# Loads of delta * u regrouped by partition quarters, and B multiplied half a unit ahead

## The chip, the cores and the metric

The kernel runs on one core of a Trainium2 chip. The metric is the device time of one execution in microseconds, as the median of several runs. The engines are TensorE (PE, with its weight loads as PEld), VectorE (DVE), ScalarE (ACT), GpSimd (POOL) and SyncE (SP). SyncE issues most of the transfers here, which sixteen DMA engines carry out.

## The reference, cut to what matters

A model of four layers. Layers 0 and 1 are selective scans over images of 64 x 64 positions with 96 channels, widened to 192 channels (E), 16 states (NS) and 4 scan directions (K), for 4 images. Layers 2 and 3 are attention and feed-forward layers on tokens, which the change doesn't touch. The core of layers 0 and 1 is, for each image, direction k and channel e:

```python
delta = softplus(einsum('bkrl,kdr->bkdl', dts, dt_w) + bias)
def step(h, inp):                       # over the L = 4096 positions
    u, d, b, c = inp
    dA = exp(d[..., None] * A)
    h = dA * h + d[..., None] * b[:, :, None, :] * u[..., None]
    y = einsum('bken,bkn->bke', h, c)
    return (h, y)
```

So for each channel and state: a decay exp(delta * A), a drive delta * u * B, a first-order recurrence along the positions, and a sum over the states with C.

## The kernel before, in words

Two images are worked on at a time (a pair), so there are four phases: two layers times two pairs. A phase consists of `prepare` (normalisation, convolution, the projections; it writes delta, delta * u, B and C to DRAM), of `scan_phase`, and of `finish` (which overlaps the next `prepare`). After the four phases, `token_layers` computes layers 2 and 3.

In `scan_phase` a partition stands for one state of one of G = 8 groups (4 directions of 2 images): 16 x 8 = 128 partitions. Partition 32a + 4g + s holds group g and state 4a + s. The free axis holds time in chunks of TC = 512 positions. The work is cut into units: one chunk and EB = 12 channels. There are 8 chunks of 16 units, 128 units in a phase, 512 in all. For each unit:

- `load` fetches delta * u from DRAM to the tile `h`, 128 x 12 x 512 in float32, each row of a group copied to all of its 16 states' partitions: 3 MB. Before, it does that in six transfers of 512 KB: three sets of four channels, each for partitions 0 to 63 and for 64 to 127 (line 390). The DRAM tensor `du` holds every row twice (its first dimension of 2), so that the source of one half has 16 different rows, each of which is read four times. `load` first calls `load_delta`, which fetches delta as three bfloat16 parts for 8 groups, 24 rows, to the tile `dlt` (line 375).
- `times_b` multiplies h by B on GpSimd, three channels at a time, four times in a unit (line 401).
- `replicate` spreads delta over the 128 partitions by a matmul to PSUM (line 407), and `decay` turns it into exp(delta * A) on ScalarE (line 411).
- `scan` runs the recurrence on VectorE for one channel, in place in h (line 418).
- `contract` sums over the states with C on TensorE (line 436), `evict` copies the sums out on ScalarE (line 448), and `store` sends them to DRAM in four transfers of 48 KB (line 456).

The order is written out by hand, and every engine executes its instructions in the order of the text. The loop goes over units and within them over the 12 channels. At channel n of unit `at` it replicates four channels ahead (LEAD), decays three ahead, scans channel n, and contracts a part of the unit before. `b_at` placed the B products of unit `at` + 1 there, one whole unit ahead. After the last channel it stores the unit before and loads unit `at` + 3; the h tiles have four buffers, so this load goes to the buffer that the unit before has just left. `weights` (line 359, ScalarE) prepares the matmul weights of the next chunk from C; `load_b` and `load_c` fetch B and C of a chunk, 16 partitions times 8 groups in four transfers of 32 partitions (line 343).

All of these transfers are issued by SyncE. At most eight are under way: each waits for the one eight issues earlier (eight completion semaphores in turn).

Of the kernel before, what the change touches and what calls it, by code (L numbers as in the profile page):

```python
# [11 lines left out]
BF16 = mybir.dt.bfloat16  # L12
# [12 lines left out]
NS = 16  # L25
R = 6
K = 4
G = 2 * K
PAD = HW + 2
TC = 512  # L30
NC = L // TC
ROWS = TC // HW
EB = 12
NEB = E // EB
ER = EB // 4
PITCH = 2
NP16 = 3
# [3 lines left out]
NF = HID // 128  # L41
EPS = 1e-5
LEAD = 4
LN_EXP = "natural_log_exp_and_others"
SQRT_HALF = 0.7071067811865476

# [33 lines left out]
class Consts:  # L80
# [3 lines left out]
    def load(self, pool, name, shape):  # L84
        t = pool.tile(shape, F32, name=name)
        self.nc.sync.dma_start(t, self.a[name])
        return t
# [39 lines left out]
class Scans:  # L127
# [19 lines left out]
    def prepare(self, ph):  # L147
# [16 lines left out]
        with self.tc.tile_pool(name="prep", bufs=1) as wp, self.tc.tile_pool(  # L164
# [3 lines left out]
            def load(name, shape, at=0):  # L168
                t = wp.tile([at + shape[0]] + shape[1:], F32, name=name)
                nc.sync.dma_start(t[at:], a[pre + name])  # L170
                return t

            xp = load("x_proj", [C, 2, 2, XD2])
            dt_w = load("dt_w", [XD2 - 2 * NS, 2, E], at=2 * NS)
            conv_b = load("conv_b", [C, 2])
            ds = load("Ds", [C, 2, K])
            dsum = wp.tile([C, 2], F32, name="dsum")
# [192 lines left out]
    def load_delta(self, u):  # L370

        nc, ph = self.nc, u.ph
        u.dl = self.units.tile([64 + NP16 * G, EB, TC], BF16, name="dlt", bufs=3)
        at = u.eb * EB
        nc.sync.dma_start(
            u.dl[64:].rearrange("p e t -> p (e t)"),
            ph.delta[u.c][:, :, at : at + EB].rearrange("n g e t -> g n (e t)"),
        )

    def load(self, u):  # L380

        nc, ph = self.nc, u.ph
        u.h = self.units.tile([128, EB, TC], F32, name="h", bufs=4)
        self.load_delta(u)
        n = 4
        for e in range(0, EB, n):
            for half in range(2):
                at = u.eb * EB + e
                part = slice(64 * half, 64 * half + 64)
                nc.sync.dma_start(  # L390
                    u.h[part, e : e + n].rearrange("p e t -> p (e t)"),
                    ph.du[u.c][:, :, at : at + n]
                    .rearrange("a g e t -> (a g) (e t)")
                    .unsqueeze(1)
                    .broadcast_to([2 * G, NS // 4, n * TC]),
                )

    def times_b(self, u, r):
        h = u.h[:, ER * r : ER * r + ER]
# [3 lines left out]
    def replicate(self, u, n):  # L403

        u.a[n] = self.p_a.tile([128, TC], F32, name="a")
        rep = self.cst.rep[64 : 64 + NP16 * G]
        self.nc.tensor.matmul(u.a[n], rep, u.dl[64:, n], start=True, stop=True)  # L407

    def decay(self, u, n):
        at = u.eb * EB + n  # L410
# [50 lines left out]
    def scan_phase(self, ph):  # L461

        nc = self.nc
        units = [self.Unit(ph, c, eb) for c in range(NC) for eb in range(NEB)]
        last = len(units)

        def ahead(t, do):
            at, n = divmod(t, EB)  # L470
            if at < last:
                do(units[at], n)

        def b_at(t):
            at, n = divmod(t, EB)
            if n % ER == 0 and 0 <= at + 1 < last:
                self.times_b(units[at + 1], n // ER)

        with self.tc.tile_pool(name="units", bufs=2) as self.units, self.tc.tile_pool(
            name="p_a", bufs=6, space=PSUM  # L480
        ) as self.p_a, self.tc.tile_pool(name="p_y", bufs=2, space=PSUM) as self.p_y:
            with self.tc.manual_schedule():
                self.start_phase(ph)
                self.load_b(ph, 0)
                self.load(units[0])
                self.load_c(ph, 0)
                self.load(units[1])
                self.load(units[2])
                self.load_c(ph, 1)
                for t in range(-EB, 0, ER):  # L490
                    b_at(t)
                for op in range(16):
                    self.weights(ph, 0, op)
                for t in range(LEAD):
                    ahead(t, self.replicate)
                for t in range(LEAD - 1):
                    ahead(t, self.decay)
                for at, u in enumerate(units):
                    before = units[at - 1] if at else None
                    for n in range(EB):  # L500
                        t = at * EB + n
                        ahead(t + LEAD, self.replicate)
                        ahead(t + LEAD - 1, self.decay)
                        self.scan(u, n)
                        q, part = divmod(n, 3)
                        if before:
                            if part < 2:
                                self.contract(before, q, part)
                            else:
                                self.evict(before, q)  # L510
                            if n == 4 and before.c < NC - 1:
                                e = before.eb * EB
                                nc.scalar.copy(
                                    ph.carry[:, e : e + EB], before.h[:, :, TC - 1]
                                )
                        b_at(t)
                        if n == 1 and u.eb >= 2 and u.c + 1 < NC:
                            self.weights(ph, u.c + 1, u.eb - 2)
                        if n == 7 and u.eb >= NEB - 2 and u.c + 1 < NC:
                            self.weights(ph, u.c + 1, u.eb)  # L520
                        if n == EB - 1:
                            if before:
                                self.store(before)
                            if u.eb == 8 and u.c + 1 < NC:
                                self.load_b(ph, u.c + 1)
                            if u.eb == NEB - 1 and u.c + 2 < NC:
                                self.load_c(ph, u.c + 2)
                            if at + 3 < last:
                                self.load(units[at + 3])
                for q in range(4):  # L530
                    self.contract(units[-1], q, 0)
                    self.contract(units[-1], q, 1)
                    self.evict(units[-1], q)
                self.store(units[-1])
# [178 lines left out]
def token_layers(ctx: ExitStack, tc, cst, a, layers, x_in, x_out):  # L713
# [51 lines left out]
    def layernorm(t, cut, out, first, **quant):  # L765
# [6 lines left out]
        with ExitStack() as order:  # L772
# [4 lines left out]
            if first:  # L777
                nc.scalar.preload_act_table_set(LN_EXP)
        var = p_a.tile([128, TC], F32, name="pa")
# [199 lines left out]
```

## Time and profile before

| | |
|---|---|
| median of 3 runs | 12560.81 us (12543.26 to 12572.67) |
| the profiled execution: time, span | 12532.27 us, 12530.5 us |
| mean granted TensorE clock | 0.736 |
| busy share of the span: PE, DVE, ACT, POOL | 78%, 75%, 56%, 59% |
| the four scan phases, first to last scan | 772 to 2728, 3655 to 5582, 6517 to 8460, 9394 to 11333 us |
| bytes moved | 2491.55 MB, of them 2163.45 on SyncE's queue |

The page's second section cuts the span into 40 slices with the busy share of each engine in tenths. Its fifth section lists groups of instructions: busy time in us and mean ns of one, then the idle time of the engine just before them and what ended most of it. In a table by stage each engine has its busy us and, in brackets, its instructions; the last three columns are the granted clock, the mean busy share of the sixteen DMA engines, and GB/s. In a list of waits, "A <- B: t, n, m" says that A stood t us in total, n times and m us at most, until B was done.

### The profile page before, as it was taken

To read this page: it belongs to the slowest core of one execution; us is meant where nothing else is said; L and a number is where in the kernel's file an instruction comes from. 1 tells how busy PE (TensorE), PEld (TensorE's weight loads), DVE (VectorE), ACT (ScalarE), POOL (GpSimd) and SP (SyncE) were. 2 spreads that over 40 slices of the span, in tenths; PEclk is the share of its full clock that TensorE was granted. 3 is DMA by queue.
4 is the path that set the end of the run, shared out by engine and by line. 5 is a ranking of instruction groups with operands and counts; after the bars stand their busy time and mean duration, and the time that the engine had idled before them with its cause. 6 is when DMAs were issued, how large, how long until landed. Compare 5 with 4: busy or idle time off the path is not lost.

```text
span 12530.5 us, 341384 instructions
## 1 busy us (share of the span) xinstructions
PE 9786.3 (78%) x147008; PEld 4985.2 (40%) x147008; DVE 9408.2 (75%) x9235; ACT 7029.5 (56%) x11815; POOL 7413.5 (59%) x2316
## 2 busy tenths in 40 slices
PE   7757788769878878869877788877877878777777
PEld 2224444433334444433334444443334444444333
DVE  2479999972569999982569999992459999994567
ACT  2356666643456666653456666662446666663456
POOL 0159888860149999870139989880118999991000
PEclk8667766679777776769777776768776676778887
DMA  3689999974679999984579999994569999994100
GB/s 93 174 223 246 239 240 242 241 183 130 201 210 248 246 248 242 243 204 125 179 206 246 244 244 245 241 227 126 159 203 236 246 245 245 246 241 134 32 21 10
DMA packets 964628, 2491.55 MB, mean 199 GB/s; under 512 B 295442, under 2 KB 578224, under 8 KB 753840
## 3 DMA queue, kind: packets, MB, share of 16 engines
q1 hardware_dynamic: 634416, 2163.45, 66.2%
q10 hardware_dynamic: 328704, 306.26, 8.4%
q8 instruction: 1158, 18.97, 0.7%
q14 instruction: 350, 2.87, 0.1%
HBM read 1955.42 MB, written 513.80 MB: 197 GB/s over the span
## 4 chain that ended last, share of the span: by engine, by line
PE 31%; DMA 28%; issue 6%; DVE 5%; SPq 4%; ACT 4%; POOL 1%; ACTq 0%; DVEq 0%; POOLq 0%
DMA h<-du 24%; PE y L436 8%; PE c L259 6%; PE a L407 5%; SPq L390 3%; PE f L586 3%; PE d L305 2%; DMA yk<-y 1%; DVE h L418 1%; PE c L288 1%; PE f L595 1%; PE f L677 1%; PE f L666 1%; PE f L652 1%; PE ph L796 1%
## 5 line engine op out<-in xcount | busy, mean ns | idle before, releaser
L401 POOL TENSOR_TENSOR h<-h,b 128x1536 f32<-128x1536 f32 x2048 | 7042.6, 3462 | 842.1 <-DMA h<-du 671.6
L418 DVE TENSOR_TENSOR_SCAN h<-a,carry,h 128x512 f32<-128x512 f32 x5376 | 6395.7, 1263 | 444.3 <-POOL h L401 329.1
L411 ACT ACTIVATE a<-a,a_col 128x512 f32<-128x512 f32 x6144 | 3939.7, 663 | 1677.4 <-PE a L407 1613.9
L436 PE MATMUL y<-h,cw 128*32 128x48 f32 x131072 | 3861.9, 268 | 1187.5 <-issue 964.3
L436 PEld LDWEIGHTS y<-h,cw 128*32 128x32 f32 x131072 | 2911.6, 138 | 3714.1 <-issue 2317.7
L407 PE MATMUL a<-dlt,rep 24*128 24x512 bf16 x6144 | 2857.7, 509 | 562.5 <-DVE h L418 466.5
L319 POOL CAST parts<-dl 96x1024 bf16<-96x1024 f32 x256 | 342.7, 1353 | 3094.3 <-DVE dl L316 2812.7
L448 ACT COPY d<-y 128x384 f32<-128x384 f32 x2048 | 980.4, 479 | 1028.8 <-PE y L436 940.8
L315 DVE TENSOR_TENSOR du_sb<-dl,xc 96x1024 f32<-96x1024 f32 x256 | 396.5, 1575 | 1292.3 <-ACT dl L313 1235.0
L259 PE MATMUL c<-xn,taps 96*96 96x512 f32 x2304 | 1034.7, 610 | 73.0 <-DVE xn L244 70.5
L418 DVE TENSOR_TENSOR_SCAN h<-a,h 128x512 f32<-128x512 f32 x768 | 863.5, 1204 | 202.7 <-ACT a L411 188.3
L407 PEld LDWEIGHTS <-rep 24*128 24x128 bf16 x6144 | 456.2, 98 | 880.6 <-issue 498.9
L305 PE MATMUL d<-xd,dt_w 7*96 7x512 f32 x1024 | 520.9, 857 | 246.5 <-ACT xd L291 220.1
L259 PEld LDWEIGHTS c<-xn,taps 96*96 96x96 f32 x2304 | 382.6, 167 | 707.8 <-issue 629.5
L818 POOL MEMSET tn<- 1x4096 f32 x8 | 28.1, 3533 | 863.6 <-PE pa L838 508.4
L586 PE MATMUL f<-yk,perm 128*128 128x384 f32 x1024 | 421.4, 552 | 92.7 <-DMA yk<-y 86.6
L266 ACT ACTIVATE xc<-c,conv_b 96x512 f32<-96x512 f32 x128 | 87.3, 682 | 721.0 <-PE c L259 661.0
L320 DVE TENSOR_TENSOR parts<-dl,parts 96x1024 bf16<-96x1024 f32 x256 | 364.8, 1446 | 155.0 <-POOL parts L319 153.4
L313 ACT ACTIVATE dl<-d 96x1024 f32<-96x1024 f32 x256 | 251.9, 1017 | 402.0 <-DMA delta<-parts 230.4
L288 PE MATMUL c<-xc,x_proj 96*103 96x512 f32 x512 | 421.6, 960 | 4.2 <-ACT xc L266 4.2
L305 PEld LDWEIGHTS d<-xd,dt_w 7*96 7x96 f32 x1024 | 151.6, 212 | 536.7 <-ACT xd L291 290.3
L359 ACT ACTIVATE cw<-c,gmask 128x256 f32<-128x256 f32 x512 | 287.1, 572 | 120.8 <-DMA h<-du 61.9
(114 smaller groups left out, 5656.4 us busy)
## 6 DMA issues: line engine op xcount, KB each, us to landing
h<-du SPq DMA_DIRECT2D x3072, 512.0 KB
delta<-parts ACTq DMA_DIRECT2D x512, 288.0 KB
dlt<-delta SPq DMA_DIRECT2D x512, 288.0 KB
du<-du_sb SPq DMA_DIRECT2D x256, 384.0 KB
du<-du_sb ACTq DMA_DIRECT2D x256, 384.0 KB
y<-d SPq DMA_DIRECT2D x2048, 48.0 KB
yk<-y SPq DMA_DIRECT2D x256, 384.0 KB
ud<-xu ACTq DMA_DIRECT2D x128, 192.0 KB
```

Of the source, the lines that this page charges most:

```text
L259: nc.tensor.matmul(rows(ps[:C]), taps[:, tap, h * C : (h + 1) * C], xn[:, ROWS * c + dy : ROWS * (c + 1) + dy, dx : dx + HW], start=tap == ...
L288: nc.tensor.matmul(rows(ps[:XD2]), xp[:, k, h], u[:, h], start=h == 0, stop=h == 1)
L305: nc.tensor.matmul(ps[:, m], dt_w[part, k, m * C : (m + 1) * C], xd[part], start=True, stop=True)
L315: nc.vector.tensor_tensor(rows(du), rows(delta), u, ALU.mult)
L390: nc.sync.dma_start(u.h[part, e : e + n].rearrange("p e t -> p (e t)"), ph.du[u.c][:, :, at : at + n] .rearrange("a g e t -> (a g) (e t)") ...
L401: self.nc.gpsimd.tensor_tensor(h, h, b, ALU.mult)
L407: self.nc.tensor.matmul(u.a[n], rep, u.dl[64:, n], start=True, stop=True)
L411: self.nc.scalar.activation(u.a[n], u.a[n], AF.Exp, scale=u.ph.a_col[:, at : at + 1])
L418: self.nc.vector.tensor_tensor_scan(u.h[:, n], u.a.pop(n), u.h[:, n], 0.0 if u.c == 0 else u.ph.carry[:, at : at + 1], ALU.mult, ALU.add,)
L436: self.nc.tensor.matmul(view(u.y[32 * j : 32 * j + 32], l2 * EB, (8 * EB, 4), (1, EB)), u.ph.cw[u.c][:, l1, 8 * j + l2], view(u.h, 64 * l1 ...
L448: self.nc.scalar.copy(u.d[:, :, :, l1], u.y[:, : 32 * EB].rearrange("p (t h x) -> p t h x", t=4, h=2))
L586: nc.tensor.matmul(ps[:, : 4 * C].rearrange("p (w v e) -> p w v e", w=4, v=nv), cst.perm[:, k], view(t, off, (sw if k < 2 else -sw, 4), (1 ...
```

## The change

Three things change. `load` fetches the first six channels of a unit in three transfers: partitions 32 to 95 (16 source rows, 768 KB), then 96 to 127 and 0 to 31 (8 source rows and 384 KB each); and the last six channels in two of 768 KB, partitions 64 to 127 and 0 to 63. A quarter reads the one copy of `du`, a pair of quarters both. `dlt` lies in partitions 0 to 23 instead of 64 to 87. And `b_at` names the unit half a unit (B_LEAD = 6 channels) ahead.

```diff
+B_LEAD = EB // 2
...
-        u.dl = self.units.tile([64 + NP16 * G, EB, TC], BF16, name="dlt", bufs=3)
+        u.dl = self.units.tile([NP16 * G, EB, TC], BF16, name="dlt", bufs=3)
...
-            u.dl[64:].rearrange("p e t -> p (e t)"),
+            u.dl.rearrange("p e t -> p (e t)"),
...
-        n = 4
-        for e in range(0, EB, n):
-            for half in range(2):
-                at = u.eb * EB + e
-                part = slice(64 * half, 64 * half + 64)
-                nc.sync.dma_start(
-                    u.h[part, e : e + n].rearrange("p e t -> p (e t)"),
-                    ph.du[u.c][:, :, at : at + n]
-                    .rearrange("a g e t -> (a g) (e t)")
-                    .unsqueeze(1)
-                    .broadcast_to([2 * G, NS // 4, n * TC]),
-                )
+        n = EB // 2
+        for first, quarters in ((1, 2), (3, 1), (0, 1)):
+            self.load_quarters(u, 0, n, first, quarters)
+        for first in (2, 0):
+            self.load_quarters(u, n, n, first, 2)
+
+    def load_quarters(self, u, e, n, first, quarters):
+
+        at = u.eb * EB + e
+        copies = slice(0, 2) if quarters == 2 else slice(first % 2, first % 2 + 1)
+        source = u.ph.du[u.c][copies, :, at : at + n]
+        self.nc.sync.dma_start(
+            u.h[32 * first : 32 * (first + quarters), e : e + n].rearrange("p e t -> p (e t)"),
+            source.rearrange("a g e t -> (a g) (e t)")
+            .unsqueeze(1)
+            .broadcast_to([quarters * G, NS // 4, n * TC]),
+        )
...
-        rep = self.cst.rep[64 : 64 + NP16 * G]
-        self.nc.tensor.matmul(u.a[n], rep, u.dl[64:, n], start=True, stop=True)
+        rep = self.cst.rep[: NP16 * G]
+        self.nc.tensor.matmul(u.a[n], rep, u.dl[:, n], start=True, stop=True)
...
-            at, n = divmod(t, EB)
-            if n % ER == 0 and 0 <= at + 1 < last:
-                self.times_b(units[at + 1], n // ER)
+            at, n = divmod(t + B_LEAD, EB)
+            if n % ER == 0 and 0 <= at < last:
+                self.times_b(units[at], n // ER)
...
-                for t in range(-EB, 0, ER):
+                for t in range(-B_LEAD, 0, ER):
                     b_at(t)
```

## The prediction, made before the changed kernel ran

> **What bounds the kernel now.** I read the page's sections 2, 3 and 5 first. They show four equal stretches in which transfers, VectorE and GpSimd are all nearly full; these are the four scan phases.
>
> ```profile
> DVE  2479999972569999982569999992459999994567
> ...
> POOL 0159888860149999870139989880118999991000
> ...
> DMA  3689999974679999984579999994569999994100
> ...
> L401 POOL TENSOR_TENSOR h<-h,b 128x1536 f32<-128x1536 f32 x2048 | 7042.6, 3462 | 842.1 <-DMA h<-du 671.6
> L418 DVE TENSOR_TENSOR_SCAN h<-a,carry,h 128x512 f32<-128x512 f32 x5376 | 6395.7, 1263 | 444.3 <-POOL h L401 329.1
> ...
> L407 PE MATMUL a<-dlt,rep 24*128 24x512 bf16 x6144 | 2857.7, 509 | 562.5 <-DVE h L418 466.5
> ...
> h<-du SPq DMA_DIRECT2D x3072, 512.0 KB
> dlt<-delta SPq DMA_DIRECT2D x512, 288.0 KB
> y<-d SPq DMA_DIRECT2D x2048, 48.0 KB
> ```
>
> A unit (12 channels, one chunk; 512 in all) needs 4 x 3.46 = 13.85 us of GpSimd and, in the trace's start times, 13.4 us of VectorE in the first chunk of a phase and 14.1 in the others: many units take exactly that. The phases, first scan to last, took 1957, 1927, 1943 and 1939 us, so a unit takes 15.17 on the mean. VectorE is idle for what is over, and GpSimd, which feeds it, waits for `h<-du`.
>
> Next the table by stage for the full part of each phase, and the waits of VectorE, SyncE's queue and TensorE in the first of them (us in total, times, longest).
>
> ```profile
> 800.00:2720.00 1920.00, 1528.57 (x33534) 825.28 (x33526) 1779.90 (x1504) 1244.42 (x2225) 1719.83 (x500) 0.70 0.95 240
> 3684.00:5574.00 1890.00, 1512.69 (x33526) 820.29 (x33525) 1775.83 (x1505) 1240.38 (x2225) 1715.17 (x499) 0.72 0.95 244
> ```
>
> ```profile
> DVE h L418 <- POOL h L401: 86.1, 116, 3.1
> DVE h L418 <- ACT a L411: 49.0, 59, 2.9
> ```
>
> ```profile
> SPq L390 <- DMA h<-du: 406.4, 325, 3.0
> SPq L456 <- DMA h<-du: 269.4, 220, 3.0
> SPq L375 <- DMA h<-du: 171.3, 111, 2.7
> ```
>
> ```profile
> PE y L436 <- issue: 256.6, 140, 4.0
> PE a L407 <- DVE h L418: 83.8, 151, 3.4
> ```
>
> The DMA share is 0.95 and the SyncE queue stands for 847 of 1920 us behind earlier loads: the transfers set the pace, by a small margin over the scans. TensorE, at a granted clock of 0.70, is close behind: its only spare time is the 84 us in which it waits for VectorE to hand back a buffer.
>
> **Working out a unit's transfers.** In the landing records of the trace each `h` load and each store posts sixteen completions, each `dlt` load (8 groups in its source) and each `c` load (32 partitions, 8 groups) eight, beside one posted at once. So an `h` load runs on 16 DMA engines, 4 rows each, and `dlt` on eight, 3 rows each. By the packet records of 800 to 2720 us, 8 KB packets (`h`) take 309 ns at the quick end, 522 on the mean and about 620 at the slow edge, twice the quick one; 12 KB packets (`dlt`) 460 and 665; the 768 B ones of the stores 43. Per engine and unit: `h` 24 x 0.522 = 12.5; `dlt` on its eight 3 x 0.665 = 2.0; stores 16 x 0.043 = 0.7; completions, instruction fetches and `b`, `c` 0.5. The eight engines carry 15.7 us in a unit of 15.2 (packets overlap a little), the others 13.6. The eight are the bound.
>
> **Part 1, the split of `h`.** Bytes stay (3 MB a unit). Six loads become five: one of 64 rows on 16 engines, two of 32 rows with 8 groups in the source, so on eight engines like `c`, and two of 64 rows. If those are the same eight that carry `dlt` (landings don't name engines; I take it so, the worse case), each of them now has 4+4+4+4+4+3 = 23 packets of 12 KB and each of the others 12. That is 21% more bytes for the busiest engines, 276 KB against 228. What can pay for it is the packet time. Alone, 23 x 0.460 = 10.6, and with the 1.2 of small terms 11.8 us. The other engines have 12 x 0.460 = 5.5 us of packets; if each of these slowed one of the eight for its whole length, 17.3. Break-even with 15.7 is 3.9 of the 5.5 us, 70% sharing. Now: (522-309) x 24 = 5.1 of a possible 7.4 us, 69%. So with today's sharing on all three loads the change is worth nothing. But the load to partitions 32 to 95 has a different layout: if its rows don't meet each other, only two thirds of the 5.5 us are exposed, 0.69 x 3.7 = 2.5, and the eight need 14.3. Scaled by 15.17/15.7 the transfers' period lies between 13.9 and 15.2; I take 14.5, the middle, because that load may still meet other loads when the eight fall behind.
>
> Two rules of the Trainium skill stand behind this, one on each side. "SBUF — State Buffer", Door 1: partitions 32 apart share a DMA port, those 64 apart don't. By it a half load puts two engines on each of 8 ports and the middle load one on each of 16; the doubling from 309 to 620 ns agrees, the middle load no run here shows yet. By this rule alone the sum is 14.3. "DMA: Bandwidth & Descriptors", Why a DMA increments its semaphore by 16: the engine count is the largest up to 16 that divides both outer dimensions, and the lowest numbered are used. It speaks against the change: quarters and `dlt` pile on the same eight, and by it alone, at today's mean packet rate, the eight need 15.7 x 276/228 = 19 us.
>
> **Part 2, `dlt` to partitions 0 to 23.** Same 24 rows, bytes and matmul shape (L407, 509 ns): nothing for TensorE. Which loads the three packets meet changes: between 3 x 0.460 and 3 x 0.920, -0.6 to +0.8 us around today's 2.0, inside the range above.
>
> **Part 3, B half a unit ahead.** In the scan phases L401 is all that GpSimd executes, 512 times in a row in both programs and in the same order. It waits for loads, not for scans, so a later place in the text moves nothing: 0. What moves is what it waits for: the first three channels need six loaded instead of four, the next three six instead of eight. A load is issued two units (30 us) before its scans, which covers the 2.5 us (one sixth of a unit's transfers); uncovered it would cost that once a phase, not per unit.
>
> **Part 4, start of a phase.** The first scan waits 34 to 36 us for ScalarE, whose `weights` wait for `c`, which is queued behind the first load. The eight engines hold 48 KB more there, at 276 KB in 14.5 us 2.5 us: 4 x 2.5 = +10 (0 to +16). SyncE issues 10 instead of 11 transfers a unit at about 0.6 us, beside its waits: 0.
>
> **The sum.** With 14.5 us of transfers VectorE's 337 us behind L401 could go. Of its 289 behind `a`, the four starts are 141, so 148 (0.3 a unit) remain from TensorE, and a faster VectorE eats TensorE's spare 84 us a phase; at low clock there is none. I let a third of the 337 return as waits for `a`: -225 + 10 = -215, a unit of 14.7. The profiled execution took 12532.3 (span 12530.5, 1.8 around it), 28.5 under the median: 12560.8 - 215, about 12345.
>
> **Rivals.**
> - *The eight engines become the queue (slower).* Place: the two quarter loads and `dlt`. From 70% sharing on, each further 10% adds 0.55 us a unit, 270 us in 508 units. At 85% 12560 + 400 = 12960; at 100% 17.3 scales to 16.7 us a unit, about 13350. For it: 21% more bytes, and they are the bound already. Against: the others then have half the work of the eight and can share for at most 5.5 us.
> - *TensorE takes over (little gain).* Busy plus waits for issue are 1785 of 1920 us, and a denser program could lower the granted clock. Then a unit stays near 15.0: -85, 12475.
> - *Transfers vanish from the path.* All 337 and half of the 148 go: -411, 12150.
> - *Nothing changes*, as with today's sharing: 12560.
>
> **How the numbers follow.** The forecast, 12280 to 12420 and its neighbourhood, has 0.46; vanished transfers 0.10; TensorE 0.12: together faster by over 0.2% (25 us, about what a measurement can tell) 0.68. No change 0.08. Slower 0.24, a third of it below 12640, since sharing just over 70% costs little. The range runs from 12140 to 12640; it leaves out some 0.03 below and 0.16 above.
>
> **What would show it.** The DMA share of the full part falls to about 0.8 in either case, since eight engines idle between loads. Right: VectorE's wait for L401 well under 337, its wait for `a` up, 12 KB packets on the eight near 0.60 us ((14.5 x 15.7/15.17 - 1.2) / 23), units near 14.7. Wrong: waits for L401 above 337 and 12 KB packets on the eight above 0.63 us (the break-even); or a quarter load that posts sixteen completions.

## The result and the profile after

| | before | after |
|---|---|---|
| median of the compared runs | 12556.23 us | 12846.87 us (12827.49 to 12876.88) |
| ratio, 95% interval | | 1.0233, 1.0208 to 1.0259 |
| span of the profiled execution | 12530.5 us | 12858.3 us |
| mean granted TensorE clock | 0.736 | 0.634 |
| mean unit of the four phases | 15.17 us | 15.74 us |

The change made the kernel slower by 2.3%. The forecast was 12345 with a range up to 12640; the time lies 207 us above the range and on the side of the first rival.

The page after, with the same parts as before. L401, L418, L407, L390, L375, L456 and L436 of before are L407, L424, L413, L397, L376, L462 and L442 now.

```profile
DVE  2478888872568888882468898992459898984566
...
POOL 0168888860148888870128888880118888882000
...
DMA  3678888864668888874568888884568888884110
...
L407 POOL TENSOR_TENSOR h<-h,b 128x1536 f32<-128x1536 f32 x2048 | 7013.8, 3454 | 1183.7 <-DMA h<-du 581.3
L424 DVE TENSOR_TENSOR_SCAN h<-a,carry,h 128x512 f32<-128x512 f32 x5376 | 6363.9, 1260 | 746.9 <-POOL h L407 737.6
...
L413 PE MATMUL a<-dlt,rep 24*128 24x512 bf16 x6144 | 3415.6, 573 | 959.3 <-DVE h L424 855.7
...
h<-du SPq DMA_DIRECT2D x1536, 768.0 KB
h<-du SPq DMA_DIRECT2D x1024, 384.0 KB
```

The three rows show mostly 8 where the phases showed 9: nothing took the place of the transfers, all of it runs slower. The products and the scans cost what they did (3454 and 1260 ns), but GpSimd's idle time rose from 842 to 1184 us, and the scans' waits for it are now most of their idle time. The table by stage (two phases) says the same:

```profile
800.00:2720.00 1920.00, 1593.15 (x32362) 806.36 (x32361) 1707.43 (x1451) 1244.60 (x2157) 1647.36 (x482) 0.54 0.82 232
3770.00:5690.00 1920.00, 1598.02 (x32641) 811.86 (x32634) 1721.29 (x1462) 1249.87 (x2171) 1661.33 (x486) 0.55 0.82 234
```

In the same 1920 us VectorE did 1451 instructions instead of 1504. The DMA share fell from 0.95 to 0.82, and yet the bytes per second fell too, from 240 to 232 GB/s. So the sixteen engines idle more and the transfers still set the pace: the lists of waits of that window, VectorE's, SyncE's queue and TensorE's, show it.

```profile
DVE h L424 <- POOL h L407: 206.7, 108, 5.7
```

```profile
SPq L397 <- DMA h<-du: 532.9, 310, 4.1
SPq L376 <- DMA h<-du: 279.8, 108, 4.2
```

```profile
PE a L413 <- DVE h L424: 201.0, 402, 4.5
PE y L442 <- issue: 56.3, 56, 4.1
```

SyncE's queue stands longer behind earlier loads: 533 instead of 406 us ahead of an `h` load, 280 instead of 171 ahead of `dlt`. Ahead of the stores it fell from 269 to 83; with the loads of `b` and `c` it is 987 us instead of 905 in all. VectorE's wait for the product rose from 86 to 207 us, and its wait for `a` (49 us before) is gone from the list. TensorE, whose granted clock fell from 0.70 to 0.54, waits for VectorE 201 us instead of 84: it moved away from the path although it became slower.

**Where the 328 us of span went.** 512 units times 15.742 less 15.167 us are 294; the rest lies outside the phases. From the scans' start times, by the place of a unit in its chunk (chunks 1 to 7), two places stand out. These are the units two after the one whose end issues `load_b` or `load_c`: 18.3 and 18.4 us, where before they took 15.6 and 16.0. The fourteen others rose from 15.18 to 15.49. Each part is worth about 0.3 us in the mean unit.

### The profile page after: what moved, and what is told of

It is laid out like the page before. It is cut to its first block, busy times and chain, and to the rows that moved or that the text cites. A ratio compares the mean times of both kernels' runs of the same rounds, so it can differ in the third digit from the quotient of the medians.

```text
span 12858.3 us, 339896 instructions
## 1 busy us (share of the span) xinstructions
PE 10300.9 (80%) x147008; PEld 5039.0 (39%) x147008; DVE 9383.5 (73%) x9235; ACT 7188.9 (56%) x11815; POOL 7384.0 (57%) x2316
## 4 chain that ended last, share of the span: by engine, by line
DMA 54%; PE 22%; DVE 7%; SPq 5%; ACT 4%; issue 4%; POOL 2%; ACTq 1%; DVEq 0%; POOLq 0%
DMA h<-du 48%; PE c L260 8%; SPq L397 4%; DVE h L424 3%; PE f L592 2%; PE y L442 2%; PE d L306 2%; PE a L413 2%; DMA yk<-y 1%; POOL h L407 1%; PE c L289 1%; DMA y<-d 1%; PE f L683 1%; PE f L601 1%; PE f L672 1%
## 5 line engine op out<-in xcount | busy, mean ns | idle before, releaser
L407 POOL TENSOR_TENSOR h<-h,b 128x1536 f32<-128x1536 f32 x2048 | 7013.8, 3454 | 1183.7 <-DMA h<-du 581.3
L424 DVE TENSOR_TENSOR_SCAN h<-a,carry,h 128x512 f32<-128x512 f32 x5376 | 6363.9, 1260 | 746.9 <-POOL h L407 737.6
L417 ACT ACTIVATE a<-a,a_col 128x512 f32<-128x512 f32 x6144 | 4016.0, 662 | 2173.6 <-PE a L413 2014.0
L442 PEld LDWEIGHTS y<-h,cw 128*32 128x32 f32 x131072 | 2937.0, 147 | 3798.8 <-issue 1962.9
L442 PE MATMUL y<-h,cw 128*32 128x48 f32 x131072 | 3799.3, 269 | 587.9 <-issue 344.3
L413 PE MATMUL a<-dlt,rep 24*128 24x512 bf16 x6144 | 3415.6, 573 | 959.3 <-DVE h L424 855.7
L424 DVE TENSOR_TENSOR_SCAN h<-a,h 128x512 f32<-128x512 f32 x768 | 869.1, 1201 | 227.8 <-ACT a L417 110.3
L413 PEld LDWEIGHTS <-rep 24*128 24x128 bf16 x6144 | 480.5, 102 | 1044.1 <-issue 556.1
```

Source lines behind the costliest of these rows:

```text
L407: self.nc.gpsimd.tensor_tensor(h, h, b, ALU.mult)
L413: self.nc.tensor.matmul(u.a[n], rep, u.dl[:, n], start=True, stop=True)
L417: self.nc.scalar.activation(u.a[n], u.a[n], AF.Exp, scale=u.ph.a_col[:, at : at + 1])
L424: self.nc.vector.tensor_tensor_scan(u.h[:, n], u.a.pop(n), u.h[:, n], 0.0 if u.c == 0 else u.ph.carry[:, at : at + 1], ALU.mult, ALU.add,)
L442: self.nc.tensor.matmul(view(u.y[32 * j : 32 * j + 32], l2 * EB, (8 * EB, 4), (1, EB)), u.ph.cw[u.c][:, l1, 8 * j + l2], view(u.h, 64 * l1 ...
```

## The experiments

The theories in the expectations: EIGHT, the engines that carry the quarters and `dlt` have too many bytes; SIZE, larger loads cost; CLOCK, `dlt` at partitions 0 to 23 lowers the granted clock and that sets the time; BURST, the first six channels now need more packets before B; MEETING, engines that write partitions of the same half slow each other, and the order of the loads decides which meet; ORDER, the order of the loads sets how far the eight engines lag and so what they meet.

I also use the landing records: for every load, the mean time of its last eight landings, and the interval from the load before it (units without `b` or `c` loads). Summed over a unit, these intervals are the pace of the slower eight engines. The mean time of a load's first eight landings says in the same way where the other eight are.

### One part at a time

```diff
 # half loads of six channels in the kernel before (e1_halves6)
-        n = 4
+        n = EB // 2
```

> Theories. EIGHT: the quarter loads pile bytes on the eight DMA engines that also carry dlt, and one of these is the last to land. SIZE: larger loads under eight outstanding transfers, and B waiting for six channels instead of four, let the queue run dry. CLOCK: dlt in partitions 0 to 23 changes TensorE's work, seen as the granted clock of 0.54 against 0.70 in the full part. This kernel is the one before with h in four half loads of six channels (no quarters, dlt where it was). EIGHT: no slower than before, 12350 to 12560 us, since the eight carry 228 KB as before in fewer packets. SIZE: 12700 to 12850. CLOCK: 12560.

12651.27 us, 1.0093 (1.0064 to 1.0123); unit 15.34. The 12 KB packets took 778 ns, 1.49 times the 522 ns of 8 KB ones: the rate did not fall. Larger transfers, with the product waiting for six channels instead of four, cost 0.9%. VectorE's wait for L401 stayed (87 us in the window); TensorE's waits for issue rose from 257 to 332 us. Which of them carries the 0.9% is open.

```diff
 # dlt at partitions 0 to 23 in the kernel before (e2_dlt_at_0)
 ...
-            u.dl[64:].rearrange("p e t -> p (e t)"),
+            u.dl.rearrange("p e t -> p (e t)"),
 ...
-        rep = self.cst.rep[64 : 64 + NP16 * G]
+        rep = self.cst.rep[: NP16 * G]
```

> The kernel before with only dlt moved to partitions 0 to 23. EIGHT: 12560 to 12700, the bytes per engine are unchanged but the three dlt packets meet other loads. SIZE: 12560. CLOCK: about 12850 and a mean granted clock near 0.63.

12697.07 us, 1.0121 (1.0099 to 1.0143). `dlt`'s 12 KB packets took 791 ns in the window instead of 665. The table by stage has the clock at 0.63 instead of 0.70, with the DMA share at 0.96:

```profile
800.00:2720.00 1920.00, 1547.78 (x32989) 820.37 (x32993) 1752.86 (x1481) 1232.90 (x2191) 1692.47 (x493) 0.63 0.96 237
```

The place of `dlt` is not shown as the cause of this clock. The window of e3, which leaves `dlt` alone, has 0.77, and of the whole executions measured side by side all but the first of each kernel lie at 0.756 to 0.763 here and at 0.762 to 0.772 in the kernel before.

```diff
 # B half a unit ahead in the kernel before (e3_b_half)
 ...
-            at, n = divmod(t, EB)
-            if n % ER == 0 and 0 <= at + 1 < last:
-                self.times_b(units[at + 1], n // ER)
+            at, n = divmod(t + B_LEAD, EB)
+            if n % ER == 0 and 0 <= at < last:
+                self.times_b(units[at], n // ER)
 ...
```

> The kernel before with only the place of the B product in the text moved to half a unit ahead. GpSimd's own order is the same, so all three theories say 12560 within 25 us. If the place matters after all: over 12600.

12560.64 us, 1.0019 (0.9999 to 1.0040): nothing, as the prediction had it.

```diff
 # the changed kernel with dlt back at 64 to 87 (e4_after_dlt_64)
 ...
-            u.dl.rearrange("p e t -> p (e t)"),
+            u.dl[64:].rearrange("p e t -> p (e t)"),
 ...
-        rep = self.cst.rep[: NP16 * G]
+        rep = self.cst.rep[64 : 64 + NP16 * G]
```

> The changed kernel with dlt back in partitions 64 to 87. EIGHT: 12750 to 12950, the eight carry the same 276 KB. SIZE: about 12850. CLOCK: back to about 12560 and a mean granted clock near 0.73.

```profile
800.00:2720.00 1920.00, 1469.07 (x32094) 785.58 (x32093) 1692.59 (x1438) 1216.60 (x2140) 1632.38 (x477) 0.72 0.83 230
```

12928.02 us, 1.0306 (1.0285 to 1.0327). The clock came back, 0.72 instead of 0.54, and the kernel was slower than the changed one (1.0233). CLOCK falls: the low clock is not the cause of the loss. The loss is in the split of `h`.

### More quarters, and the loads between

```diff
 # both sets of six channels by middle and quarters (e5_quarters_twice)
-        for first, quarters in ((1, 2), (3, 1), (0, 1)):
-            self.load_quarters(u, 0, n, first, quarters)
-        for first in (2, 0):
-            self.load_quarters(u, n, n, first, 2)
+        for e in (0, n):
+            for first, quarters in ((1, 2), (3, 1), (0, 1)):
+                self.load_quarters(u, e, n, first, quarters)
```

> Both sets of six channels in the middle load and two quarters. EIGHT (the eight engines that carry the quarters and dlt are full, and their packets are shared as much as before): they have 27 packets of 12 KB instead of 23, 17% more; the free time alone is 12.4 + 1.2 us, with the other engines' 8 packets shared at 70% 16.2: 12900 to 13300 us, and the DMA share falls below 0.8. BURST (the loss is the first half's long way, 15 packets on the eight before B can start, felt after the extra loads of B and C): the second half gets the same way, at most as slow as the first: 12850 to 13000.

13057.93 us, 1.0404 (1.0376 to 1.0433), DMA share 0.70. The eight have 27 packets, and the mean packet took 601 ns instead of 688. More bytes on the eight cost more even at faster packets, so there is something in EIGHT.

```diff
 # the changed kernel, load_b and load_c behind the unit's own load (e6_after_bc_behind)
+                            if at + 3 < last:
+                                self.load(units[at + 3])
 ...
-                            if at + 3 < last:
-                                self.load(units[at + 3])
```

> The changed kernel with the four loads of B or of C issued behind a unit's load instead of ahead of it. In the changed kernel the units two after these loads take 18.3 us, the others 15.5 (before: 15.9 and 15.2). BURST: the long units fall to about 15.7, 12700 us. EIGHT: the loads' bytes are the same, they only move: 12800 to 12850.

12857.17 us, 1.0246 (1.0220 to 1.0272). The two long units only moved one place on (18.0 and 18.1 us). BURST had them fall to 15.7, which they did not. What makes them long is the four small loads in a row, not their place ahead of the unit's own load.

### The order of the loads

```diff
 # halves for the first six channels, middle and quarters for the last six (e9_after_quarters_last)
-        for first, quarters in ((1, 2), (3, 1), (0, 1)):
-            self.load_quarters(u, 0, n, first, quarters)
-        for first in (2, 0):
-            self.load_quarters(u, n, n, first, 2)
+        for first in (2, 0):
+            self.load_quarters(u, 0, n, first, 2)
+        for first, quarters in ((1, 2), (3, 1), (0, 1)):
+            self.load_quarters(u, n, n, first, quarters)
```

> The changed kernel with the order of the two sets turned: halves for the first six channels, the middle load and the quarters for the last six. The bytes on each engine are the same. EIGHT: 12800 to 12900. BURST: B's first channels come after 11 packets on the eight instead of 15, so the long units shrink by half: about 12750.

12541.12 us, 0.9992 (0.9972 to 1.0012): the whole loss is gone, with the same transfers, the same bytes on every engine and the same TensorE work. Neither EIGHT nor BURST had expected that. The table by stage and VectorE's first wait of the window:

```profile
800.00:2720.00 1920.00, 1575.96 (x33987) 832.78 (x33986) 1778.81 (x1516) 1272.52 (x2238) 1714.23 (x501) 0.65 0.81 241
```

```profile
DVE h L424 <- POOL h L407: 124.4, 89, 4.7
```

At the same DMA share (0.81 and 0.82) 241 GB/s are moved instead of 232. The intervals of the slower eight in us, in the order of issue (the stores of `y`, about 1.0 in all, left out):

| kernel | loads of `h` | `dlt` | sum with stores |
|---|---|---|---|
| before | six of 1.87 to 2.16, sum 12.18 | 1.65 | 14.8 |
| after | middle 2.31, quarter 96-127 **2.82**, quarter 0-31 **3.07**, half 64-127 2.34, half 0-63 2.23 | 1.73 | 15.4 |
| e9 | half 64-127 3.06, half 0-63 2.80, middle 1.96, quarter 96-127 **1.77**, quarter 0-31 **2.05** | 1.95 | 14.5 |

A quarter alone needs 4 packets of 460 ns, 1.84 us. In e9 the quarters run almost alone. In the changed kernel, while the eight are in quarter 96-127, the other eight have done their part of the middle load and go on with half 64-127; the later part of quarter 0-31 runs beside half 0-63. Quarters and half loads meet in the same half of the partitions. The landings, in us from that of `dlt`, in units away from `b` and `c` loads: the other eight end the middle load at 0.4, half 64-127 at 6.6 and half 0-63 at 9.8; the eight are in quarter 96-127 from 2.3 to 5.0 and in quarter 0-31 from 5.0 to 8.0.

```diff
 # the changed kernel with its last two loads exchanged (e15_after_halves_swapped)
-        for first in (2, 0):
+        for first in (0, 2):
```

> The changed kernel with only its last two loads exchanged: partitions 0 to 63 ahead of 64 to 127. MEETING: in the changed kernel the eight's quarter load of partitions 96 to 127 runs while the other eight engines write the half 64 to 127, and their quarter 0 to 31 while the others write 0 to 63; so the quarters take 2.8 and 3.1 us between landings (1.8 alone). Exchanged, each quarter runs beside the other half: the quarters fall to about 2 us, ordinary units to about 14.6, 12450 to 12620 us. BURST (the first half's long way before B): the order of the first six channels is unchanged, 12800 to 12870.

12751.75 us, 1.0146 (1.0125 to 1.0167). A gain of 95 us, where the expectation of MEETING had at least 227. Quarter 96-127 now has half 0-63 beside it and took 2.24 instead of 2.82. Quarter 0-31 took 2.94; by the expectation it should have met half 64-127, and it did not gain. The landing records show why it met half 0-63 instead: counted as above, quarter 0-31 runs from 4.7 to 7.7, and the other eight, which end the middle load at 0.8, end half 0-63 only at 7.7. So quarter 0-31 still meets a load of its own half, and quarter 96-127 no longer does. The long units fell to 16.2 and 16.5 us.

```diff
 # e9 with its first two loads exchanged (e22_quarters_last_swapped)
-        for first in (2, 0):
+        for first in (0, 2):
```

> The kernel with the quarters last, its first two loads exchanged: 0 to 63 ahead of 64 to 127. The bytes and the set order stay. ORDER: the half loads took 3.1 and 2.8 us between landings, which this moves by up to 0.5 us each: 12350 to 12800. A time within 25 us of 12541 speaks for no influence of the halves' order.

```profile
800.00:2720.00 1920.00, 1500.55 (x30340) 760.13 (x30344) 1607.46 (x1359) 1174.92 (x2035) 1542.31 (x451) 0.53 0.85 217
```

13441.18 us, 1.0706 (1.0675 to 1.0737). The exchange of two entries of a list, with no byte moved to another engine, costs 900 us against e9. Quarter 0-31 and `dlt` at 0-23, the last on the eight, are now followed by half 0-63 of the next unit, which the other eight, done with the middle load, can begin at once: 2.49 and 2.53 us instead of 2.05 and 1.95. The largest part is elsewhere, in the unit's second load of `h`: half 64-127 took 3.4 us, where half 0-63 took 2.80 in that place. Why is open.

```diff
 # e9 with dlt at 64 to 87 (e21_quarters_last_dlt_64)
 ...
-            u.dl.rearrange("p e t -> p (e t)"),
+            u.dl[64:].rearrange("p e t -> p (e t)"),
 ...
```

> The kernel with the quarters last, with dlt back in partitions 64 to 87, where the first half load also goes. ORDER (the order of loads sets how far the eight lag and so what they meet; the bytes stay): dlt's three packets meet the first half, +0.4 us a unit as from the changed kernel to its version with dlt at 64, 12650 to 12750 us. If dlt's place counts only beside quarters first: 12540.

12849.30 us, 1.0219 (1.0174 to 1.0263). `dlt` is followed by half 64-127 here, the half that it now lies in, and takes 2.71 us instead of 1.95.

For `dlt`, on eight engines with a half load behind it, the runs line up:

| | kernel before: `dlt` at 64, half 0-63 behind | e9: at 0, half 64-127 behind | e2: at 0, half 0-63 | e22: at 0, half 0-63 | e21: at 64, half 64-127 |
|---|---|---|---|---|---|
| same half | no | no | yes | yes | yes |
| `dlt`, us | 1.65 | 1.95 | 2.20 | 2.53 | 2.71 |

With a middle load behind it, which touches both halves, `dlt` took 1.73 us at 0 to 23 (the changed kernel) and 2.3 at 64 to 87 (e4). The halves alone don't explain that difference.

### The meeting by itself

The kernel before, with series of eight loads appended behind its end, each series by itself, into a tile that nothing else uses (its time includes them, so it is not compared). An entry gives the first quarter of the partitions and the number of quarters.

```diff
+        for plan in (
+            [(0, 2)] * 8,
+            [(1, 2)] * 8,
+            [(0, 1)] * 8,
+            [(0, 2), (2, 2)] * 4,
+            [(0, 1), (0, 2)] * 4,
+            [(0, 1), (2, 2)] * 4,
+        ):
+            for i, (first, quarters) in enumerate(plan):
+                load(i, first, quarters)
```

> The kernel before, with six series of eight loads each behind its end, into a tile that nothing uses (12 KB rows, at most eight under way, a pause between series): eight times partitions 0 to 63; eight times 32 to 95; eight times 0 to 31 (eight groups); 0 to 63 and 64 to 127 in turn; 0 to 31 and 0 to 63 in turn; 0 to 31 and 64 to 127 in turn. MEETING (engines slow each other where their rows are in partitions that share a port): 12 KB packets of about 0.92 us in the first series and 0.46 in the second and third, 0.92 in the fourth if all engines keep step; in the fifth the eight engines' packets over 0.6 us, in the sixth nearer to 0.46 when the other engines have run ahead. If memory or the whole core's rate is the limit: the first and second series alike, since both ask for the same bytes from sixteen engines.

The table by stage, one line for each series in the order of the list; the engines' columns are all but empty, the last three are clock, DMA share and GB/s.

```profile
12545.70:12578.60 32.90, 0.00 (x0) 0.00 (x0) 0.00 (x0) 0.00 (x0) 0.00 (x0) 0.50 0.92 191
12579.20:12597.30 18.10, 0.00 (x0) 0.00 (x0) 0.00 (x0) 0.00 (x0) 0.00 (x0) 0.50 0.86 348
12597.70:12615.30 17.60, 0.00 (x0) 0.00 (x0) 0.00 (x0) 0.00 (x0) 0.00 (x0) 0.50 0.43 179
12615.70:12647.20 31.50, 0.00 (x0) 0.00 (x0) 0.00 (x0) 0.00 (x0) 0.00 (x0) 0.50 0.91 200
12647.60:12673.00 25.40, 0.00 (x0) 0.00 (x0) 0.01 (x1) 0.00 (x0) 0.00 (x0) 0.50 0.76 186
12673.40:12694.70 21.30, 0.00 (x0) 0.00 (x0) 0.00 (x0) 0.00 (x0) 0.00 (x0) 0.50 0.72 222
```

Half 0-63 (first line) and middle 32-95 (second) carry the same bytes on sixteen engines: 191 against 348 GB/s, 946 ns a packet against 483 in the packet records, from which the other packet times here are too. A quarter on eight engines (third) moves 179 GB/s: a half load on sixteen is hardly faster than a quarter on eight. Alternating halves (fourth) gain little, 894 ns. The last two lines are the question of this case: quarters 0-31 with half loads between, in the same half (801 ns, 25.4 us) and in the other (633 ns, 21.3 us). Same bytes on the same engines; the meeting costs 19%.

### Small loads spread, and dlt on twelve engines

```diff
 # e9 with the b and c loads one a unit over four units (e16_quarters_last_spread)
 ...
-                            if u.eb == 8 and u.c + 1 < NC:
-                                self.load_b(ph, u.c + 1)
-                            if u.eb == NEB - 1 and u.c + 2 < NC:
-                                self.load_c(ph, u.c + 2)
+                            if 5 <= u.eb < 9 and u.c + 1 < NC:
+                                self.load_b(ph, u.c + 1, [u.eb - 5])
+                            if 12 <= u.eb and u.c + 2 < NC:
+                                self.load_c(ph, u.c + 2, [u.eb - 12])
```

(`load_b` and `load_c` are changed to load the parts that they are given.)

> The kernel with the quarters last, and the four loads of B and of C no longer together but one in each of four units. In that kernel the units after these loads take 17.4 us, the others 14.9. If four small transfers in a row leave the eight engines without work (at most eight transfers are under way, and four stores are among them), the long units go: -2.4 us in two of 16 units, 150 us, about 12390. If their bytes or their own time count: 12520 to 12560.

12715.94 us, 1.0127 (1.0096 to 1.0158): slower, which neither expectation had. The long units are gone (15.6 and 15.7 instead of 17.4 and 17.3), but the others rose from 14.96 to 15.59 on the mean.

The same edit in the kernel before (e17_before_spread):

> The same spreading alone, in the kernel before, whose units after these loads are 0.8 us longer than the others, twice over two units: 1.6 us in two of 16 units at most, 100 us: 12440 to 12520; 12540 if the bytes count.

12728.23 us, 1.0124 (1.0099 to 1.0149), slower against the expectation too: 8 KB packets took 543 ns instead of 522. And with e15's order (e18_swapped_spread):

> The changed kernel with the halves exchanged and the loads of B and C spread. MEETING plus the spreading: 12350 to 12480 us. BURST: 12650 to 12750.

12559.86 us, 1.0002 (0.9983 to 1.0020): here it gained, 1.4% against e15, though not down to the 12350 to 12480 expected of MEETING. So a burst of small loads does two things: it holds up one unit, and it seems to set anew how far the eight engines lag behind the others. The landings go with that: from the mean of a half load's first eight landings to that of its last eight lie 1.67 us in e16's first half load (e9: 2.06) and 1.47 in e17's (before: 1.78), but 3.06 in e18's half 0-63 (e15: 2.67). The two that lost lag less, the one that gained lags more. That the lag makes the time is a reading: e4 lags more than the changed kernel (4.8 against 4.0 us in half 64-127) and is slower.

```diff
 # dlt of the kernel before as one dimension of 24 rows (e10_dlt_12)
-            ph.delta[u.c][:, :, at : at + EB].rearrange("n g e t -> g n (e t)"),
+            ph.delta[u.c][:, :, at : at + EB].rearrange("n g e t -> (n g) (e t)"),
```

(The constant `rep` is reordered to match.)

> The kernel before with the 24 rows of dlt in the order of the DRAM tensor (part by part instead of group by group; the replicating matrix is turned to match), so that rows of source and tile make one dimension of 24. If the engine count is the largest up to 16 that divides both, twelve engines carry two rows each instead of eight three, and each landing posts twelve. EIGHT: the busiest engines lose one 12 KB packet a unit, 0.67 us of 15.7: 12250 to 12480 us. If another limit sets the pace (all sixteen, or the one engine that is always last): 12500 to 12560.

```profile
800.00:2720.00 1920.00, 1470.89 (x32150) 793.81 (x32154) 1708.58 (x1442) 1184.07 (x2141) 1646.45 (x480) 0.67 0.98 231
```

12952.66 us, 1.0322 (1.0299 to 1.0346). It posted twelve completions, so the busiest engines have fewer bytes, and the kernel lost, outside both expectations: the DMA share rose to 0.98 and the rate fell to 231 GB/s, with 8 KB packets at 556 ns instead of 522. One reading is that engines that keep in step meet in every half load (the first eight and last eight landings of the first half load lie 1.48 us apart, 1.78 before). But the scans of this window did not wait for the product of GpSimd:

```profile
DVE h L418 <- ACT a L411: 177.5, 163, 3.7
...
DVE h L418 <- POOL h L401: 13.9, 14, 3.9
```

```profile
PE y L436 <- issue: 415.9, 188, 4.2
```

They waited for `a` (49 us before), and TensorE, whose matmul starts each `a`, stood 416 us for issue (257 before). The packet records say for what: each of its 173 stops of over 0.5 us for issue ended 1.1 to 1.8 us behind the end of a 16 KB instruction packet, where 9% of evenly spaced times lie. TensorE waited for its own instructions, which come through the same full DMA engines. So spreading the same bytes over more engines lost 3% here, with late instructions on the path of the scans; how much of it is the meeting in half loads is not shown.

The same edit of `dlt` in e9 (e23_quarters_last_dlt_12) and in e18 (e24_swapped_spread_dlt_12):

> The kernel with the quarters last, with dlt on twelve engines as in e10. By bytes alone the eight lose one 12 KB packet of 23 a unit, 0.5 to 0.6 us of their 14.5: about 12400 us. If what dlt does to the lag between the two groups of engines counts for more, as in e10 (where 0.67 us of bytes less made the unit 0.8 us longer): 12600 to 12950.

```profile
800.00:2720.00 1920.00, 1563.17 (x34062) 832.69 (x34061) 1793.93 (x1548) 1271.32 (x2246) 1715.74 (x501) 0.67 0.84 243
```

12406.81 us, 0.9891 (0.9860 to 0.9922): faster than both kernels, as the count of bytes had it. (This phase ends at 2676 us, so the window holds 44 us of what follows.) VectorE's wait for the product is 90.0 us. Unit 14.90, the long ones still 16.7 and 17.2.

> The same on the changed kernel with the halves exchanged and the loads of B and C spread (12560 us). Bytes: about 12400. Lag: 12600 to 12950.

12697.02 us, 1.0124 (1.0093 to 1.0155), within the range that was expected of the lag, and 1.2% behind e18. Its scans waited for the product (160 us), and half 0-63 has its first and last eight landings 2.41 us apart, 3.06 in e18. Quarter 0-31 took 3.33 us instead of 2.94, and the halves 2.72 and 2.96 instead of 2.29 and 2.38.

## Why the prediction was wrong

**What bounds the kernel: right.** The transfers set the pace, in both kernels, and VectorE's waits for L407 rose with them. That the DMA share would fall to about 0.8 in either case was right too (0.82), which is why the share was no sign of anything. The sign of being wrong did come: 817 us of waits for the product over the execution, where 337 was the bound.

**Part 1, the term that failed.** The working had the break-even at 70% sharing, 3.9 of the 5.5 us of packets of the others. It then exposed only the half loads, two thirds of them, at today's 69%: 2.5 us, a sum of 14.3. That mean exposure is a property of an order, not of a set of loads. In the order of e9 the slower eight spent 11.64 us in `h` loads against 20 packets x 0.460 = 9.2 alone, 2.4 us of exposure, and the sum of their intervals was 14.5; the prediction had 2.5 and 14.3. That they are so near is in part luck: `dlt` had 0.6 us of exposure more (1.95 against 1.38 alone), and the stores came to 0.9 where 1.2 of small terms stood in the sum. In the order of the change the same packets took 12.77 us, an exposure of 3.6, because quarters of the eight ran beside halves of the others. On the prediction's own scale an ordinary unit of 15.49 us is 15.49 x 15.7/15.17 = 16.0 us for the eight, 4.2 us above 11.8 and so 76% of 5.5 us; 12 KB packets on the eight are then (16.0 - 1.2)/23 = 0.64 us, just over the 0.63 that it named as the sign of being wrong. I wrote that the middle load might still meet others "when the eight fall behind" and paid 0.6 us for it (14.5 against the 13.9 at the quick end); I did not write out which load runs beside which when they do.

What stands behind this is Door 1 of the Trainium skill's "SBUF — State Buffer": 32 apart shares a port. The appended series agree (946 ns against 483), and so does the prediction's use of it for the middle load; it was the quarters to which I did not apply it. From the rule "Why a DMA increments its semaphore by 16" in "DMA: Bandwidth & Descriptors" the engine counts came out as expected, eight completions for a quarter and twelve for a `dlt` of one dimension of 24. The 19 us that this rule gives by itself, at a fixed packet rate, is far off, since the packets got faster: 688 ns for 12 KB, where 522 for 8 KB would make 783.

**Not in the sum: the long units.** 2.8 us in two of sixteen units is 0.36 us in the mean. The kernel before has them hardly (0.4 to 0.8 us above the rest, 0.08 in the mean), so the growth is about half of the loss of 0.575. The runs show that they come from the small loads of `b` and `c` (e6 moves them, e16 removes them) and that the order of the half loads changes them (e15). Four such loads post eight completions each, so each of eight engines has 4 x 4 packets of 2 KB, at 104 ns 1.7 us; the prediction had spread this over all units, within its 0.5 us for `b`, `c` and the rest. The other 1.1 us, and why the kernel before shows less than the 1.7, were not settled. e9 has them too (17.4 and 17.3), and they eat its gain: its other units are at 14.96, its mean at 15.17.

**Part 2, `dlt`: counted at nothing, worth one or two percent of either sign.** +1.2% in the kernel before (e2). In the changed kernel the same move brought the ratio from 1.0306 (e4) to 1.0233, -0.7%, and in e9's order from 1.0219 (e21) to 0.9992, -2.2%. The bounds of -0.6 to +0.8 us a unit held, the middle was no estimate.

**Part 3: right**, nothing (e3).

**Part 4, the starts: right.** VectorE's waits at the four starts were 141 us; all its waits for `a` and for `h` loads come to 113.2 + 38.2 = 151, so at most +10.

**A third of 337 us returns as waits for `a`: wrong in its direction.** TensorE was close to the path before; a slower feed took it away, and its clock of 0.54 did not bring it back. Its waits for issue, which the rival of TensorE counts as if they were its work (1785 of 1920 us), fell from 257 to 56 us with the DMA share, so they belonged to the transfers too. In e9, with the transfers at 14.5 us, the only wait of the scans in the window's list was that for the product.

**The rivals.** *The eight engines become the queue* is what happened, at its mild end; by its price (0.55 us a unit for 10%) the 0.31 us of the ordinary units are 6 points of sharing. The 76% above comes from the same units by the same scale, so this is no test of the price. It had a good mechanism and too small a chance, because the case against it ("the others have half the work") says for how long they can share, not whether they do. *TensorE takes over* and *transfers vanish* fall.

**What stays open.** How the lag between the two groups of engines settles, and how much of the time it makes; the long units; the second load in e22; `dlt` behind a middle load; and what larger loads cost by themselves (e1, 0.9%).

## What to carry to other kernels

When transfers run on different numbers of DMA engines, don't stop at the bytes per engine: write down which transfer the idle engines go on to, and whether it writes the same half of the partitions as the one that the busy engines are in. The landing records say which loads really ran together; in e15 they were not those that the order of issue suggested. A share of sharing measured in one order does not hold in another, so run the few orders there are: here the order alone was worth 7%. Balancing the engines is no aim in itself; twelve engines instead of eight for `dlt` cost 3.2% and 1.2% in two orders (e10, and e24 against e18) and gained 1.0% in a third (e23 against e9).

## What the runs showed of the hardware that I had not expected

- A load to partitions 0 to 63 on sixteen engines moved 191 GB/s, one to 32 to 95 with the same bytes 348, and one to 0 to 31 on eight engines 179.
- The granted TensorE clock is not the kernel's alone: whole executions of the kernel before had 0.69 to 0.77. Nor did it follow the place of `dlt`: with `dlt` moved back to 64 to 87 the window had 0.72 instead of 0.54 in the changed kernel's order (e4), and 0.60 instead of 0.65 in e9's (e21). e4 at 0.72 was slower than the changed kernel at 0.54.
- What the profile lists as TensorE's wait for issue was a wait for instructions: in the window every such stop of over 0.5 us ended 1.1 to 1.8 us behind the end of a 16 KB instruction packet, 120 stops in the kernel before, 173 in e10, 41 in the changed kernel. They came to 252 and 412 us at DMA shares of 0.95 and 0.98, and to 53 at 0.82.
- Levelling the engines raised the DMA share from 0.95 to 0.98 and lowered the rate from 240 to 231 GB/s.
